# In_proj as 32x128 tiles beside ssm_out, one pair further ahead, with the first half's silus brought to their partitions by a staging tile and SBUF transfers

## The chip, the cores and the metric

The kernel runs on one NeuronCore of a Trainium2 chip, as one launch. The metric is device time in microseconds, the median of several executions. Before the change it is 1737.05 us (three runs, 1736.68 to 1737.44). Everything is float32.

## The reference

Four images x of 128 channels and 96x96 pixels are normalized in groups of four channels. Each is then read as four sequences of L = 9216: by rows, by rows backwards, by columns, by columns backwards. Every sequence goes through the same block (HID 256, MH 32, K 5, G 4):

```python
t = _grouped1x1(x, in_proj_w, in_proj_b, G)        # 128 -> 512 channels, 4 groups of 32 inputs
u, gate = (t[:, :HID], t[:, HID:])
u = jax.nn.silu(u)
u = lax.conv_general_dilated(u, dw_w, ...)          # depthwise, 5 taps
s = _conv1x1(u, ssm_in_w)                           # 256 -> 32
a = clip(DMIN + (DMAX - DMIN) * sigmoid(_conv1x1(u, ssm_delta_w, ssm_delta_b)), ...)
bb = tanh(_conv1x1(u, ssm_b_w, ssm_b_b)); cc = tanh(_conv1x1(u, ssm_c_w, ssm_c_b))
# h[l] = a[l] * h[l-1] + bb[l] * s[l], written with cumsums
u = u + _conv1x1(cc * hst + ssm_d[None, :, None] * s, ssm_out_w)     # 32 -> 256
u = _grouped1x1(u * jax.nn.sigmoid(gate), mix_w, mix_b, G)
return _conv1x1(u, out_proj_w, out_proj_b)          # 256 -> 128
```

The four results are put back in image order, joined to 512 channels, multiplied by fuse_w (512 to 128) and added to x. The kernel folds mix, out_proj and fuse into one matrix for each direction (w_fin), whose products it adds into the image, acc.

## The kernel before

**Order of work.** There are eight phases: four images, each once with columns as sequences (order V), once with rows (order H). A phase runs a sequence and its reverse together (s = 0, 1) in NS = 6 *steps* of 1536 positions, and a step in R = 4 *pairs*, one for each residue p of the position modulo 4, in the order TURN = 1, 2, 3, 0. So there are 192 pairs of 384 positions in two sequences; t numbers them, and a phase has 24. Since the second sequence is the first one backwards, the last three steps of a phase need the same in_proj and gates as the first three, mirrored. Only the first three are computed (fresh(step)); the others read what was kept, in SBUF (steps 3 and 4 use the silus of 2 and 1) or in DRAM (the gates, and the silus of step 0).

**A pair.** `pair_on(t)` writes the instructions of all engines by hand, in the order in which each engine runs them; the first six pairs have a function of their own, `pair(t)`. A pair holds, on TensorE: the depthwise conv of the first 128 channels as matmuls (`conv` with the matrices band, 128 rows by 32 columns, and in pairs of residues 1 and 2 also `conv_less`, 64 rows); two products with w_fin (`accumulate`) for a pair some seven back; the four ssm_out matmuls (`out_of`, L577) of the pair six back, 32 rows by 128 columns; and the projections to bb, cc, a and s (`proj`, 16 matmuls of 128 by 32). VectorE does the five taps of the other 128 channels (`taps`), the recurrence and the gating. GpSimd multiplies for the recurrence and adds into acc. ScalarE evaluates and copies out of PSUM.

**The front.** in_proj for four pairs ahead (a *front*, the g-th of the four of its step) stands at the start of a pair, `front(t + R, FRONT)`: for both sequences and both halves (j = 0, channels 0 to 127, for the conv; j = 1, the others, for the taps) four matmuls of 32 rows by 32 columns, 16 in all, and four silus (L527) into `sil`, whose first half has a residue on each 32 partitions. Column tile c of a matmul writes partitions 32c to 32c + 31 of the result; for j = 0 the four tiles are the four residues of channel group g, so the silus come out where the conv wants them; for j = 1 they are the four channel groups of residue g. Pairs with t modulo 24 from 20 to 7 hold a front; I call them *fronted*. The other twelve (8 to 19) hold the gates: four matmuls of 32 rows by 128 columns (`gate`, L557) between those of ssm_out, then a narrow tanh for each of two (L593, L599), and a wide one of both sequences.

**PSUM.** Eight banks. Taps and ssm_out use 0 to 3. In a gated pair conv uses 6 and 7, the products and projections 4 and 5 (PROJ). In a fronted pair the front uses 7, 6, 2, 3, conv 4 and 5, the products 7 and 6 (`banks, w`).

**Transfers.** Nearly all transfers are issued by SyncE, in the order of the program, each as soon as what it waits for is done; they go round eight semaphores, and one waits for the last transfer on its own. x_in is loaded for a front one step ahead (`load_front`), kept gates two pairs ahead (`load_kept`). `keep_lone` stores the outer residues of a step's silus (edge_sil), which `load_lone` brings back at the start of the step for `add_lone`. `keep_silu` (L507) stores the silus of step 0 for step 5. The pool gives `sil` two buffers, so step 2 takes that of step 0. `shared` has one buffer.

## Time and profile before

| | before |
|---|---|
| median of the runs | 1737.05 us |
| the profiled execution, its span | 1735.2 us |
| DMA engines busy, hardware queue 1 | 62.8% of 16 |
| moved | 363.66 MB, 210 GB/s |
| busiest TensorE groups | w_fin products 541.3 us, projections 535.0 us, conv 285.3 us, ssm_out 228.1 us, gates 161.7 us |
| silus, L527 | 384, 191.6 us, 584 ns each |

A profile shows one execution. TensorE's busy time counts pipelined matmuls, four of 32 columns side by side, so a busy TensorE can still hold pauses; how long a pair takes is better read between two starts of an instruction that comes once in each pair, as L781, the tanh of the projections.

### The profile page before, as it was taken

Reading aid. Unit: us, or ns where it says so; the run is one execution under the profiler, and the core shown is the slowest. Engines: PE = TensorE matmul, PEld = TensorE weight load, DVE = VectorE, ACT = ScalarE, POOL = GpSimd, SP = SyncE. Lnnn points to the kernel's source line nnn. Section 1 sums busy time; section 2 is a strip of 40 time slices with the busy share of each in tenths; the row PEclk is TensorE's granted clock in tenths of the full one; section 3 lists DMA queues with packets and bytes.
Section 4 is the critical chain, followed back from the end, with each engine's and each line's share of the span. In section 5 each row is a group of like instructions: output and inputs, shape, how many; then the busy total and the mean of one; then the engine's idle time right before and its main releaser. Section 6 shows DMA issues by size and latency. Waiting matters only on the chain.

```text
span 1735.2 us, 54226 instructions
## 1 busy us (share of the span) xinstructions
PE 1713.6 (99%) x22522; PEld 644.7 (37%) x22522; DVE 1507.9 (87%) x1508; ACT 1494.8 (86%) x2544; POOL 1447.0 (83%) x1490
## 2 busy tenths in 40 slices
PE   7999999999999999999999999999999999999998
PEld 4333333343333433344333443334333333333333
DVE  6899998888889998888889999888888888888887
ACT  4888988889888888888988888888998889888875
POOL 3689889888789988888788988887878889887887
PEclk9999999999999999999999999999999999999999
DMA  7746865358884786337896487433887548643364
GB/s 244 235 147 218 288 202 151 124 206 280 275 287 139 262 267 194 118 126 263 260 308 226 150 300 251 144 123 132 294 294 239 179 144 304 201 137 133 147 226 166
DMA packets 154644, 363.66 MB, mean 210 GB/s; under 512 B 19104, under 2 KB 120864, under 8 KB 154400
## 3 DMA queue, kind: packets, MB, share of 16 engines
q1 hardware_dynamic: 154256, 360.16, 62.8%
q8 instruction: 178, 2.92, 0.7%
q14 instruction: 66, 0.54, 0.1%
q10 hardware_dynamic: 144, 0.04, 0.0%
HBM read 221.41 MB, written 138.53 MB: 207 GB/s over the span
## 4 chain that ended last, share of the span: by engine, by line
PE 95%; DVE 2%; ACT 1%; DMA 1%; issue 0%; SPq 0%; DVEq 0%; ACTq 0%
PE psum L130 81%; PE psum L577 8%; PE psum L557 5%; DVE psum L744 1%; PE psum L1188 0%; DMA acc<-in_xr 0%; DMA kept<-shared 0%; DVE u L638 0%; ACT psum L589 0%; ACT psum L742 0%; DVE u L744 0%; ACT sil L527 0%; SPq L335 0%; PE psum L1195 0%; DVE u L691 0%
## 5 line engine op out<-in xcount | busy, mean ns | idle before, releaser
L744 DVE SCALAR_TENSOR_TENSOR psum<-sil,small,psum 128x768 f32<-128x768 f32 x576 | 589.1, 1023 | 42.2 <-ACT psum L742 16.8
L130 PE MATMUL psum<-u,w_fin 128*32 128x384 f32 (+1 forms) x6192 | 541.3, 484 | 1.1 <-ACT ys L860 0.4
L130 PE MATMUL psum<-u,main 128*32 128x384 f32 x6144 | 535.0, 489 | 0.5 <-DVE u L691 0.4
L638 DVE SCALAR_TENSOR_TENSOR u<-gate,psum 128x768 f32<-128x768 f32 x376 | 341.7, 950 | 150.0 <-PE psum L577 50.8
L879 POOL TENSOR_TENSOR acc<-ys,acc 128x384 f32<-128x384 f32 x375 | 411.8, 1120 | 14.0 <-ACT ys L860 1.9
L825 POOL TENSOR_TENSOR t<-t,t 64x384 f32<-64x384 f32 (+1 forms) x192 | 287.2, 1496 | 70.6 <-DVE t L819 48.3
L589 ACT COPY psum<-u 128x768 f32<-128x768 f32 x384 | 301.4, 799 | 10.5 <-DVE u L638 4.3
L130 PEld LDWEIGHTS psum<-u,w_fin 128*32 128x32 f32 x6192 | 195.2, 109 | 309.6 <-issue 235.5
L130 PEld LDWEIGHTS psum<-u,main 128*32 128x32 f32 x6144 | 180.0, 109 | 324.5 <-issue 218.3
L130 PE MATMUL psum<-sil,band 128*32 128x384 f32 x3072 | 285.3, 488 | 0.0
L792 POOL TENSOR_SCALAR t<-tm 64x384 f32<-64x384 f32 x184 | 170.8, 928 | 114.4 <-ACT tm L781 102.4
L826 POOL TENSOR_TENSOR t<-t,t 64x384 f32<-64x384 f32 (+1 forms) x192 | 233.9, 1218 | 15.1
L793 POOL TENSOR_TENSOR t<-t,tm 64x384 f32<-64x384 f32 x192 | 213.8, 1113 | 30.2 <-ACT t L784 15.5
L577 PE MATMUL psum<-t,main 32*128 32x384 f32 x1536 | 228.1, 525 | 4.2 <-ACT psum L589 4.2
L742 ACT ACTIVATE psum<-sil,small 128x768 f32<-128x768 f32 x191 | 172.6, 904 | 65.2 <-DVE u L638 61.9
L744 DVE SCALAR_TENSOR_TENSOR u<-sil,small,psum 128x768 f32<-128x768 f32 x192 | 194.9, 1015 | 6.8
L527 ACT ACTIVATE sil<-psum,bnorm 128x385 f32<-128x385 f32 x384 | 191.6, 584 | 4.0 <-DMA edge<-sil 0.9
L557 PE MATMUL psum<-x_in,wn 32*128 32x384 f32 x768 | 161.7, 498 | 0.0
L862 ACT COPY ys<-psum 128x384 f32<-128x384 f32 x288 | 132.3, 478 | 33.0 <-PE psum L130 28.3
L130 PEld LDWEIGHTS psum<-sil,band 128*32 128x32 f32 x3072 | 88.8, 108 | 171.4 <-issue 63.1
L781 ACT ACTIVATE tm<-psum,small 128x384 f32<-128x384 f32 x192 | 110.9, 578 | 14.0 <-PE psum L130 2.3
L577 PEld LDWEIGHTS psum<-t,main 32*128 32x128 f32 x1536 | 93.9, 183 | 73.7 <-issue 41.0
(108 smaller groups left out, 1512.3 us busy)
## 6 DMA issues: line engine op xcount, KB each, us to landing
gate<-kept SPq DMA_DIRECT2D x114, 768.0 KB, 5.2
kept<-gate SPq DMA_DIRECT2D x74, 768.0 KB, 3.7
sil<-sil SPq DMA_DIRECT2D x64, 770.0 KB, 6.6
lone<-edge SPq DMA_DIRECT2D x40, 770.0 KB, 7.5
x_in<-in_xs SPq DMA_DIRECT2D x250, 96.2 KB, 3.3
edge<-sil SPq DMA_DIRECT2D x96, 192.5 KB, 3.6
out<-acc SPq DMA_DIRECT2D x46, 384.0 KB, 6.4
acc<-in_xr SPq DMA_DIRECT2D x39, 384.0 KB, 6.4
```

The costliest lines, as they stand in the source:

```text
L130: nc.tensor.matmul(o[r, : rhs.shape[-1]], lhsT, rhs, start=start, stop=stop, skip_group_check=True)
L527: nc.scalar.activation(sils[step][:, s, j, g, :], bank(bk)[:, : N + 1], AF.Silu, bias=bn[:, 1:2] if j else bn[:, 4 + g : 5 + g],)
L557: nc.tensor.matmul(bank(to)[:, :N], stats[un["b"]][0][r, s, :], x_in[s][r, q, off : off + N], start=True, stop=True)
L577: nc.tensor.matmul(bank(ssm(bi, s) + j)[:, :N], w_so[r, bass.ts(j, P)], z[r, :], start=(bi, s) not in seeded, stop=True, skip_group_check= ...
L589: nc.scalar.copy(psum[:, ssm(bi, s) : ssm(bi, s) + 2, :N], us[bi][:, s])
L638: nc.vector.scalar_tensor_tensor(v, g, 1.0, pz, ALU.add, ALU.mult)
L742: nc.scalar.activation(part, src, AF.Copy, scale=w_tap[:, 0:1])
L744: nc.vector.scalar_tensor_tensor(us[i][:, :, 1, :] if k == K - 1 else part, src, w_tap[:, k : k + 1], part, ALU.mult, ALU.add,)
L793: nc.gpsimd.tensor_mul(ta[0:64, p, :], tb[0:64, :], tm[0:64, :])
L825: engine.tensor_mul(ta[0:64, p, r], tb[64:P, r], ta[64:P, p, r])
L826: engine.tensor_add(tb[0:64, r], ta[0:64, p, r], tb[0:64, r])
L879: adder.tensor_add(part, y, part)
```

## The change

In_proj leaves the start of the pair. `new_front` writes it as four matmuls of 32 rows by 128 columns, one for each sequence and half, in the places between the ssm_out matmuls where a gated pair has its gates, and for the pair five ahead (`ahead = t + R + 1`). With it the fronted pairs move by one: those with t modulo 24 from 19 to 6. The gates of a phase's first pairs are shared out again, two of them (no longer three) in the pairs 17 and 18 of the phase before. All pairs now use the banks of a gated pair.

For j = 1 a matmul gives the 128 channels of residue g where the taps want them, and two narrow silus (`new_silu`, L502) write `sil`. For j = 0 it gives all four channel groups of residue g on the four groups of partitions, and the conv wants the four residues there. So one wide silu of both sequences (`new_stage`, L515) writes a staging tile, and four transfers bring channel group m from partitions 32m of staging to partitions 32g of `sil`, at m. Staging has two slots, by g % 2, in the one buffer of `shared`, taken anew for each step. The edges are stored from staging, at g = 0 and g = 3, two transfers a step where `keep_lone` had four. The biases of the old layout and their spreading (`spread`) fall away. `keep_silu` of step 0 moves to the fronts of step 1, behind the transfers out of staging.

TensorE, pair 68 (phase 2, its step 5 begins), before. x_in is the input of in_proj, wn the normalized weights; the rows u, w_fin are the products, t, main ssm_out and u, main the projections:

```order
L130 MATMUL psum<-x_in_70,wn_2589 32x385 x8
L130 MATMUL psum<-x_in_71,wn_2589 32x385 x8
L130 MATMUL psum<-sil_6561,band 32x384 x8
L130 MATMUL psum<-u_3_2_0_6295,w_fin 32x384 x16
L130 MATMUL psum<-sil_6561,less 32x384 x8
L577 MATMUL psum<-t_2_3_3_0_6447,main 128x384 x4
L130 MATMUL psum<-u_5_1_0_6968,main 32x384 x16
```

and the same pair now:

```order
L130 MATMUL psum<-sil_6265,band 32x384 x8
L130 MATMUL psum<-u_3_2_0_5999,w_fin 32x384 x8
L130 MATMUL psum<-sil_6265,less 32x384 x8
L130 MATMUL psum<-u_3_2_0_5999,w_fin 32x384 x8
L490 MATMUL psum<-x_in_70,wn_2498 128x385
L622 MATMUL psum<-t_2_3_3_0_6151,main 128x384 x3
L490 MATMUL psum<-x_in_70,wn_2498 128x385
L490 MATMUL psum<-x_in_71,wn_2498 128x385
L622 MATMUL psum<-t_2_3_3_0_6151,main 128x384
L490 MATMUL psum<-x_in_71,wn_2498 128x385
L130 MATMUL psum<-u_5_1_0_6654,main 32x384 x16
```

The sixteen small matmuls at the start have become four among those of ssm_out.

SyncE, the end of pair 74 (t modulo 24 = 2, phase 3) and the first rows of the end of pair 75, in the changed kernel. L523 are the four pieces out of staging, L526 the edge, L552 the store of step 0's silus (sil_18 is step 0 of phase 3, sil_19 step 1, sil_20 step 2), L659 a load of kept gates; a row names the semaphores that it waits for, DMAHW those of transfers, and a transfer counts on the one that it waits for:

```order
L659 DMA gate0_176<-kept0_3_181 128x1536 [waits DMAHW4_49,DVE_49]
L523 DMA sil_19_6985<-shared_7010 32x2x385 [waits DMAHW5_49,Activation_49]
L523 DMA sil_19_6985<-shared_7010 32x2x385 [waits DMAHW6_49]
L523 DMA sil_19_6985<-shared_7010 32x2x385 [waits DMAHW7_49]
L523 DMA sil_19_6985<-shared_7010 32x2x385 [waits DMAHW0_49]
L526 DMA edge1_1_214<-shared_7010 128x2x385 [waits DMAHW1_49]
L552 DMA sil1_3_209<-sil_18_6598 128x1540 [waits DMAHW2_49]
L297 DMA x_in0_70<-in_xs 64x385 [waits DMAHW3_49,PE_49]
L297 DMA x_in1_71<-in_xs 32x385 [waits DMAHW4_49,PE_49]
L297 DMA x_in1_71<-in_xs 32x385 [waits DMAHW5_49,PE_49]
L659 DMA gate1_177<-kept0_2_180 128x1536 [waits DMAHW6_49,DVE_49]
```

The store of residue 3 stands behind the four pieces and the edge of that pair, on semaphore 2. Those of residues 1 and 2, in the pairs before, are on 7 and 0. Before the change the store stood in the fronts of step 0 itself, at the start of a pair and three pairs earlier.

ScalarE, pair 75 (t modulo 24 = 3), where step 2 begins, in the changed kernel. L634 and L907 are copies of the pair, L502 the narrow silus, L787 the first tap of the next pair, L515 the wide silu, L826 the tanh of the projections:

```order
L634 COPY psum_72<-u_2_5_2_0_6755 128x2x384 [waits DVE_49]
L907 COPY ys_2_5_1_1_7391<-psum_72 128x384 [waits PE_49]
L502 ACTIVATE sil_20_7393<-psum_72,bnorm_1_2499 128x385 [waits DMAHW2_49,DMAHW7_49,DMAHW0_49,PE_49]
L502 ACTIVATE sil_20_7393<-psum_72,bnorm_1_2499 128x385 [waits PE_49]
L787 ACTIVATE psum_72<-sil_19_6985,small_91 128x2x384 [waits DVE_49]
L515 ACTIVATE shared_7408<-psum_72,bnorm_1_2499 128x770 [waits DMAHW5_49,DMAHW4_49,DMAHW6_49,DMAHW1_49,DMAHW7_49,DMAHW0_49,Activation_49]
L826 ACTIVATE tm_3_0_0_0_7432<-psum_72,small_91 128x384 [waits PE_49,Pool_49]
```

Four silus at the start of the pair have become two narrow ones and a wide one between the gatings. The first of step 2 waits for the semaphores 2, 7 and 0.

The diff, cut to its core:

```diff
@@ pair(t), the first six pairs
-            front(t + R, FRONT if banks == PROJ else (5, 4, 2, 3))
+            spots = FRONT if banks == PROJ else (5, 4, 2, 3)
+            if t < R:
+                front(t + R, spots)
+            for f in {4: (8,), 5: (9, 10)}.get(t, ()):
+                to = (4, 5, 2, 3) if banks != PROJ else (6, 7, 2, 3)
+                one = new_front(f, to)
+                for x, y in ((0, 1), (0, 0), (1, 0), (1, 1)):
+                    one(x, y)
+                new_silu(f, to)
+                new_stage(f, to)
...
@@ the front
+    def new_front(i, banks):
+        step, g = divmod(i, R)
+        if g == 0:
+            sils[step] = new_sil(step)
+        st, r = step % NS, (0, 32, 64, 96)
+        def one(s, j):
+            q = R - 1 - g if s > j else g
+            a = slice(64 * s + 32 * j, 64 * s + 32 * j + 32)
+            nc.tensor.matmul(
+                bank(banks[2 * j + s])[:, : N + 1], stats[units[step * UB]["b"]][0][a, s, :], x_in[s][a, q, :],
+                start=True, stop=True,
+            )
+        return one
+
+    def new_silu(i, banks):
+        step, g = divmod(i, R)
+        bn = stats[units[step * UB]["b"]][1]
+        for s in range(2):
+            nc.scalar.activation(
+                sils[step][:, s, 1, g, :], bank(banks[2 + s])[:, : N + 1], AF.Silu, bias=bn[:, 1:2]
+            )
+
+    def new_stage(i, banks):
+        step, g = divmod(i, R)
+        st, bn, sil = step % NS, stats[units[step * UB]["b"]][1], sils[step]
+        if g == 0:
+            stages[0] = shared()[:, : 4 * (N + 1)].rearrange("p (e s n) -> p e s n", e=2, s=2)
+        stage = stages[0][:, g % 2]
+        nc.scalar.activation(
+            stage, psum[:, banks[0] : banks[0] + 2, : N + 1], AF.Silu, bias=bn[:, 0:1]
+        )
+        if st == 0:
+            nc.gpsimd.memset(stage[:, g // 2, 0:1], 0.0)
+            if g < 2:
+                nc.gpsimd.memset(sil[:, :, 1, g, 0:1], 0.0)
+        for m in range(4):
+            nc.sync.dma_start(sil[32 * g : 32 * g + 32, :, 0, m, :], stage[32 * m : 32 * m + 32, :, :])
+        if g in (0, R - 1):
+            e = 0 if g else 1
+            nc.sync.dma_start(
+                edge_of(step)[2 * e : 2 * e + 2].rearrange("a g c n -> (g c) a n"), stage
+            )
+        if st == 1 and step > 1:
+            keep_silu(step - 1, g)
+        if st < NS // 2 - 1:
+            load_front(step + 1, 0, slice(0, 64), slice(g, g + 1))
+            load_front(step + 1, 1, slice(64, 96), slice(R - 1 - g, R - g))
+            load_front(step + 1, 1, slice(96, P), slice(g, g + 1))
...
     def after_front(step, g):
...
-        if step and step % NS == 0:
-            keep_silu(step, g)
...
@@ pair_on(t)
-        fronted, gated = fresh(step), None
-        if mirror(n + 1) is None and (n + 1) % NP > 2:
+        ahead, gated = t + R + 1, None
+        if ahead * 2 >= NU or not fresh(ahead // R):
+            ahead = None
+        if mirror(n + 1) is None and (n + 1) % NP > 1:
...
-        banks, w = (PROJ, FRONT[:2]) if fronted else ((6, 7), PROJ)
+        banks, w = (6, 7), PROJ
...
-        front(t + R, FRONT)
+        mirrored(t + R)
...
+        spots = (6, 7, 4, 5)
+        if ahead is not None:
+            one = new_front(ahead, spots)
         def gate_of(s, j, bk):
             if gated is not None:
                 gate(2 * gated, s, j, bk)
+            elif ahead is not None:
+                one(1 - s, j)
...
+            elif s == 0 and ahead is not None:
+                new_silu(ahead, spots)
...
+        if ahead is not None:
+            new_stage(ahead, spots)
```

105 lines of the change are left out of this document (40 added, 65 removed).

## The prediction

> **What bounds the kernel now.** I read the page first, from its busy shares and its chain of waits:
>
> ```profile
> span 1735.2 us, 54226 instructions
> ...
> PE 1713.6 (99%) x22522; PEld 644.7 (37%) x22522; DVE 1507.9 (87%) x1508; ACT 1494.8 (86%) x2544; POOL 1447.0 (83%) x1490
> ...
> PE 95%; DVE 2%; ACT 1%; DMA 1%; issue 0%; SPq 0%; DVEq 0%; ACTq 0%
> ```
>
> TensorE is busy for 99% of the span and carries 95% of the chain that ended last. So a stage costs what TensorE's rounds cost plus every wait that lets TensorE stand, while the other engines have 13 to 17% to spare. The profiled execution took 1735.2 us against a median of 1737.05 us of the runs: 1.9 us more, which I add at the end.
>
> Next I read the busy time by stretches, with the starts of the projection's tanh (L781, once a pair) as borders. The first row is the six whole phases from pair 24 to pair 168, the second four fronted pairs (from pair 96), the last two four gated ones each (from pairs 104 and 32); the last column but one is the DMA engines' busy share:
>
> ```profile
> 237.36:1505.80 1268.44, 1267.80 (x16780) 472.32 (x16776) 1107.40 (x1077) 1124.10 (x1915) 1085.07 (x1114) 1.00 0.65 215
> 871.97:907.60 35.63, 35.63 (x516) 12.29 (x512) 31.25 (x33) 31.93 (x56) 28.67 (x29) 1.00 0.88 291
> ...
> 943.01:977.96 34.95, 34.95 (x424) 13.98 (x416) 32.65 (x33) 30.67 (x51) 32.24 (x29) 1.00 0.45 148
> ...
> 308.40:343.10 34.70, 34.70 (x420) 13.93 (x416) 29.98 (x29) 30.50 (x51) 28.30 (x28) 1.00 0.36 121
> ```
>
> Four fronted pairs take 35.63 us, four gated ones 34.70 or 34.95, although both hold the same number of matmul rounds: the 16 in_proj tiles of 32x32 are one round, the four gates of 32x128 another.
>
> **What the change removes.** By the order of TensorE's instructions a fronted pair now reads exactly like a gated one: four 32x128 matmuls between the four of ssm_out, in the same places and against the same banks. ScalarE's order is the gated pair's too, two narrow silus and a wide one where two narrow tanhs and a wide one stood. So the gated row prices it. Six phases are 36 groups of four: 36 x 34.70 = 1249.2 us, and the row has 1268.4, so 19.2 us lie in 72 fronted pairs, 0.27 us each. 85 pairs get an in_proj ahead: 22.7 us. Some gated groups take 34.95 us, which leaves less, so I take 21 us. Bounds: 0.17 us a pair (35.63 less 34.95, over four: 14 us) and 0.27 (23 us). Cover for the rest: ScalarE loses one activation a pair and VectorE nothing, both off the path. In the head one more front is made in pair 5, one round, under 1 us.
>
> **What it adds: transfers and one late wait.** Each front adds four transfers of 96 KB from staging to sil, and at residues 0 and 3 the edge copies leave from staging (384 KB each, before four of 192 KB once a step). The nearest rows are the page's DMA issues, with KB and median us to landing:
>
> ```profile
> gate<-kept SPq DMA_DIRECT2D x114, 768.0 KB, 5.2
> ...
> x_in<-in_xs SPq DMA_DIRECT2D x250, 96.2 KB, 3.3
> edge<-sil SPq DMA_DIRECT2D x96, 192.5 KB, 3.6
> ```
>
> The gated pairs give the times allowed, in the timeline of pairs 106 and 107 (start and length, us):
>
> ```profile
> 959.66 0.89 ACT L599 ACTIVATE gate<-psum,bnorm 128x768 f32<-128x768 f32 x1
> ...
> 965.72 0.58 ACT L593 ACTIVATE gate<-psum,bnorm 128x384 f32<-128x384 f32 x1 [0.33 <-PE psum L557]
> ...
> 967.92 0.89 ACT L599 ACTIVATE gate<-psum,bnorm 128x768 f32<-128x768 f32 x1
> ...
> 969.05 0.83 PE L130 MATMUL psum<-sil,band 128*32 128x384 f32 x8
> ```
>
> The wide activation, after which the staged pieces go out, ends at 960.55. From there 5.2 us pass to the next pair's first narrow activation (965.72), 7.4 to its wide one (967.92) and 8.5 to the conv after it (969.05), the first reader of a step's last pieces. SyncE's rows of pair 46 and the line view of the store of silus (L507) show how fast transfers are issued:
>
> ```profile
> 434.80 2.71 SPq L676 DMA_DIRECT2D edge<-sil  x4
> 437.61 0.55 SPq L507 DMA_DIRECT2D sil<-sil  x1
> ...
> L507 SPq DMA_DIRECT2D sil<-sil x32: 338/345/1399, 39.7 to 1494.9; - x32
> ...
> DMA to landing us min/median/max: 3.8/5.1/7.1
> ```
>
> Four issues take 1.4 to 2.7 us (0.34 each alone, 2.71 for the four edge copies). A piece lands 3.3 to 5.2 us behind its issue, so the last at 2 + 4 = 6 us of 8.5: hidden.
>
> The store of step 0's silus (keep_silu) is not. It moved from in front of a pair to behind the staging, and from the fronts of step 0 to those of step 1, since it must wait for the staged halves. Its last piece now leaves at the end of a pair t = 2 (mod 24). One pair on, at t = 3, step 2 begins, its tile takes step 0's buffer, and its first narrow silu (L502) waits for that store. In the order of ScalarE this silu names exactly the semaphores of those stores, in 7 of the 8 phases. Before, five pairs lay between. Behind the silu stand the first tap, the wide silu and the projection's tanh of ScalarE, and TensorE's projection, which needs the banks that the silus empty: a wait there is a wait of TensorE.
>
> How late is it? In the 5.2 us the store must be issued and land. Ahead of the store stand four staged pieces and an edge copy. Five issues take 1.7 to 3.4 us; I take 2.5. Landing is 3.8 to 7.1 us after issue; behind a gate load, 384 KB of pieces and a 384 KB edge I take 6.4, near the store above that had four edges ahead. Wait: 2.5 + 6.4 - 5.2 = 3.7 us; bounds 2.5 + 3.8 - 5.2 = 1.1 and 2.5 + 7.1 - 5.2 = 4.4. That holds for the four phases of order H (1, 3, 5, 7), where DMA is light (0.50 in the first row below, pairs 24 to 27): 4 x 3.7 = 15 us.
>
> The three V phases that follow another image (2, 4, 6) are crowded: outputs leave and the next image loads. The rows behind the first are pairs 47 to 50, into phase 2:
>
> ```profile
> 237.36:273.30 35.94, 35.94 (x536) 12.38 (x528) 30.63 (x32) 31.11 (x57) 32.07 (x37) 1.00 0.50 153
> ...
> 439.40:448.73 9.33, 9.33 (x140) 3.19 (x136) 8.01 (x8) 8.41 (x15) 8.28 (x8) 1.00 1.03 319
> 448.73:458.00 9.27, 9.27 (x140) 3.13 (x136) 7.72 (x8) 8.42 (x16) 6.78 (x8) 1.00 1.04 357
> 458.00:466.52 8.52, 8.52 (x124) 2.98 (x120) 7.78 (x10) 7.55 (x14) 8.06 (x9) 1.00 0.62 232
> 466.52:475.04 8.52, 8.52 (x124) 2.98 (x120) 7.75 (x10) 7.55 (x14) 5.57 (x6) 1.00 0.84 223
> ```
>
> and, of the first two, the landing of a gate load:
>
> ```profile
> issues: line engine op xcount, KB each, median us to landing
> gate<-kept SPq DMA_DIRECT2D x3, 768.0 KB, 7.7
> ```
>
> Two stretches are full (1.03 and 1.04) at a mean of 338 GB/s. Each now gets 384 KB of pieces and a 770 KB store more, the first also an edge of 384 KB: 2.7 MB, 8 us at that rate. The third has 0.38 x 8.5 = 3.2 us free and gets 3.4 us of work. So the store of the last piece can be 8 us later than in an H phase: 3.7 + 8 = 11.7 us. The least is a store that meets only the landing times of full stretches (7.7 us), with no backlog in front: 2.5 + 7.7 - 5.2 = 5.0. I take 8.5, the middle, since shares over 1 say that transfers overlap: 3 x 8.5 = 25 us.
>
> The staging tile has one buffer, too. The wide silu of residue 0 waits for the pieces and the edge of residue 3, one pair before. At t = 23 that pair's pieces also wait for GpSimd's memset, which stands behind two accumulations (one pair's rows):
>
> ```profile
> 900.92 1.97 POOL L879 TENSOR_TENSOR acc<-ys,acc 128x384 f32<-128x384 f32 x2
> ...
> 907.43 1.96 POOL L879 TENSOR_TENSOR acc<-ys,acc 128x384 f32<-128x384 f32 x2
> ```
>
> The second ends at 909.4, 1.8 us behind the tanh L781 that starts at 907.60, about when the wide activation ends. Pieces and edge are issued by 1.8 + 2.5 = 4.3 us and land 3.6 us later, at 7.9; a pair gives 7.4. Some 0.5 us, seven times: 3 us, bounds 0 and 9.
>
> Sum: 1735.2 - 21 + 15 + 25 + 3 = 1757; with the 1.9 us of the median, **1759 us**.
>
> **A rule weighed.** The store is 770 KB, and its quickest landing was 3.8 us. By the Trainium skill (DMA: Bandwidth & Descriptors, Anatomy of one DMA) a DMA costs about 2.0 us plus its bytes over 436 GB/s, an estimate of 3.8 us here (a fit of transfers that GpSimd issues). By that price every boundary would cost 1.1 us and the change would gain: the second rival's time. The row's median of 5.1 us speaks against it, since a transfer that stands behind others takes their time too.
>
> **Rivals.** First, *the same wait, and TensorE's clock falls in it.* TensorE stood for 11.66 us at the start, and its first matmuls then went slowly:
>
> ```profile
> 11.66 5.49 PE L1188 MATMUL psum<-acc 128*128 128x512 f32 x6 [11.66 <-DMA acc<-in_xr]
> ...
> 18.05 0.57 PE L1188 MATMUL psum<-acc 128*128 128x192 f32 x2
> ```
>
> 5.49 us for 3 x 512 columns (each recorded twice) is 3.6 ns a column, against 0.57/192 = 3.0: 0.9 us lost at least, since the small ones' fixed part weighs more. At 1.3 us a wait, seven add 9 us: 1768. For it: the waits last a third of that first idle, or nearly all of it. Against: no idle in the steady part shows it. The Trainium skill (TensorE: Matmul & The Clock Gate, The HAM clock gate) puts the threshold at an idle window of about 3.4 us, so the crowded boundaries would pay and the light ones perhaps.
>
> Second, the other side: *the store lands in time.* Place: L502 at t = 3; it decides when the store's mean landing falls under some 5.7 us, where seven waits eat the 21 us. At 3.8 us each wait is 1.1 us, 8 in all: 1737 - 21 + 8 = 1724. For it: the fastest of 32 stores. Against: those had no five transfers just ahead.
>
> Third, *the wait is not met at all*, because ScalarE is itself late by then: the gain alone, 1716. It would have to be 4 us late in each fresh half, and the gated rows show it waiting for TensorE (0.33 us).
>
> Fourth, *transfers flood every fronted pair*: the conv of steps 0 to 2 waits as well, and the crowded boundaries cost 12 us or more with loads of gates late. 3 x 12 + 15 + 10 - 21 = +40: 1777. For it: shares of 1.03. Against: 0.65 over the six phases.
>
> **How the numbers follow.** Forecast 0.5, clock 0.2, flood 0.12, store in time 0.10, gain alone 0.03, waits and gain equal 0.05. The forecast's own range, from the bounds: least waits 4 + 15 + 0 less 21 gives 1735, most 18 + 35 + 9 less 21 gives 1778. The rival of the clock is inside; to leave out no more than 2 in 10 I take 1734 to 1782. Slower by over 0.2% (3.5 us, about what a measurement of this kernel can tell from none): 0.82; faster 0.13; within 0.05.
>
> **What would show it.** In the changed profile: fronted stretches without a boundary at 34.7 to 34.9 us a group (the gain); L502 preceded by idle ended by a DMA sil<-sil or by the semaphore of one, seven times, 3 to 5 us in H phases and 5 to 12 in V phases; the store's landing at 6 us or more; L515 idle at t = 23 under 1 us; no conv waiting for sil<-shared. A granted clock under 1.00 behind the waits would be the first rival. Wrong would be: no idle before L502, or group times of 35.6 as before.

## The result and the profile after

The changed kernel takes 1822.09 us (median of four runs, 1819.75 to 1827.23), 1.0496 times the kernel before (interval 1.048 to 1.0513): 85 us slower. The prediction said slower, at 1759 us, and gave 1734 to 1782 as its range: the sign is right, the size is not.

The page of the changed kernel, its span, busy shares, chain and TensorE clock (each digit of that row a fortieth of the span, in tenths):

```profile
span 1818.8 us, 50579 instructions
...
PE 1722.7 (95%) x20410; PEld 696.8 (38%) x20410; DVE 1523.4 (84%) x1508; ACT 1481.6 (81%) x2414; POOL 1450.7 (80%) x1462
...
PEclk9999999999899999999989999899998999999999
...
PE 80%; DMA 9%; ACT 3%; DVE 2%; SPq 2%; issue 2%; POOL 1%; ACTq 0%; POOLq 0%; DVEq 0%
```

TensorE's share of the chain fell from 95% to 80%, and transfers hold 9%, where they held 1%. Every engine's share fell: the kernel waits. The busy time by stretches, first the same six whole phases (pairs 24 to 167) and then the same four fronted pairs from pair 96, gives the place:

```profile
240.06:1582.42 1342.36, 1274.65 (x15048) 515.42 (x15048) 1118.77 (x1077) 1112.64 (x1807) 1087.27 (x1089) 0.97 0.71 220
904.17:955.84 51.67, 37.89 (x420) 14.57 (x416) 32.20 (x33) 31.34 (x52) 29.39 (x30) 0.83 0.96 296
```

The six phases take 73.9 us more than before (1268.44), the four pairs 51.67 instead of 35.63 us, with a granted clock of 0.83 and the DMA engines busy for 0.96. The group list names what ScalarE waited for, and the line view of the store of silus (L552) how long that took to land:

```profile
L502 ACT ACTIVATE sil<-psum,bnorm 128x385 f32<-128x385 f32 x176 | 101.6, 582 | 118.7 <-DMA sil<-sil 55.1
...
ACT sil L502 <- DMA sil<-sil: 55.1, 6, 15.8
...
ACT sil L502 <- DMA x_in<-in_xs: 16.5, 1, 16.5
...
DMA to landing us min/median/max: 4.7/7.6/9.3
```

Seven waits of the narrow silu, 71.6 us in all, at t = 3 of phases 1 to 7. The first four pairs of these phases take 79.7 us more than before (between the starts of the tanh), all the rest of the kernel 3.9 us more. One wait is booked on a load of x_in, which the silu does not read; the transfer that was last by the profile need not be the one that counted. Phase 1, in ScalarE's and TensorE's timelines and SyncE's queue:

```profile
256.55 0.89 ACT L515 ACTIVATE shared<-psum,bnorm 128x770 f32<-128x770 f32 x1
...
268.73 1.05 ACT L502 ACTIVATE sil<-psum,bnorm 128x385 f32<-128x385 f32 x2 [6.42 <-DMA sil<-sil]
...
269.37 5.35 PE L130 MATMUL psum<-u,main 128*32 128x384 f32 x32 [5.92 <-ACT sil L502]
...
257.47 2.53 SPq L523 DMA_DIRECT2D sil<-shared  x4
260.04 0.59 SPq L526 DMA_DIRECT2D edge<-shared  x1
260.68 0.49 SPq L552 DMA_DIRECT2D sil<-sil  x1
```

The pieces leave when the wide activation has ended (257.4), the store 3.2 us later; the silu starts 8.0 us after that. And in phase 2, where the tanh L826 starts as the wide activation ends:

```profile
475.78 0.57 ACT L826 ACTIVATE tm<-psum,small 128x384 f32<-128x384 f32 x1
...
496.62 1.05 ACT L502 ACTIVATE sil<-psum,bnorm 128x385 f32<-128x385 f32 x2 [15.82 <-DMA sil<-sil]
...
484.34 3.17 SPq L523 DMA_DIRECT2D sil<-shared  x4
487.55 0.59 SPq L526 DMA_DIRECT2D edge<-shared  x1
488.19 0.48 SPq L552 DMA_DIRECT2D sil<-sil  x1
```

SyncE reached the pieces 8.5 us after they were ready: it was a pair behind. The projections behind the wait in phase 1 took 5.35 us, in a pair without one 2.77:

```profile
306.92 2.77 PE L130 MATMUL psum<-u,main 128*32 128x384 f32 x32
```

The stretches behind the two waits show why, with the granted clock in the last column but two:

```profile
269.40:274.80 5.40, 5.40 (x36) 1.74 (x40) 4.08 (x4) 2.60 (x5) 0.89 (x1) 0.50 0.26 61
275.00:283.30 8.30, 8.30 (x108) 3.05 (x104) 6.21 (x4) 7.12 (x12) 7.67 (x6) 1.00 0.52 153
...
497.30:500.10 2.80, 2.80 (x20) 0.94 (x24) 1.56 (x2) 1.99 (x3) 0.00 (x0) 0.50 1.03 357
```

TensorE ran at half speed for 5.4 us in the one and 2.8 us in the other. By the same view of the other five waits it was 4.4 to 6.0 us there, 35.5 us for all seven; half of that is lost, an estimate of 18 us. The Trainium skill (TensorE: Matmul & The Clock Gate, The HAM clock gate) says that the array falls to half speed after an idle window of about 3.4 us and comes back after a busy one of that length. The trace agrees that it falls in a wait and comes back in work: in all seven waits, of 4.3 to 16.0 us on TensorE, the clock fell. It does not show the length: the fall came 1.9 us (phase 3) to 4.9 us (phase 6) after TensorE's last matmul, and the return 2.9 to 6.0 us after its next.

### The profile page after: what moved, and what is told of

Same layout as the page of the kernel before. It is cut to its first block, busy times and chain, and to the rows that moved or that the text cites. A ratio compares the mean times of both kernels' runs of the same rounds, so it can differ in the third digit from the quotient of the medians.

```text
span 1818.8 us, 50579 instructions
## 1 busy us (share of the span) xinstructions
PE 1722.7 (95%) x20410; PEld 696.8 (38%) x20410; DVE 1523.4 (84%) x1508; ACT 1481.6 (81%) x2414; POOL 1450.7 (80%) x1462
## 4 chain that ended last, share of the span: by engine, by line
PE 80%; DMA 9%; ACT 3%; DVE 2%; SPq 2%; issue 2%; POOL 1%; ACTq 0%; POOLq 0%; DVEq 0%
PE psum L130 65%; PE psum L622 6%; PE psum L602 5%; DMA sil<-sil 4%; PE psum L490 4%; SPq L523 2%; DMA edge<-shared 1%; DMA gate<-kept 1%; DMA x_in<-in_xs 1%; DVE psum L789 1%; DMA sil<-shared 1%; DVE t L864 1%; ACT psum L787 1%; DVE u L683 1%; ACT tm L826 1%
## 5 line engine op out<-in xcount | busy, mean ns | idle before, releaser
L130 PE MATMUL psum<-u,main 128*32 128x384 f32 x6144 | 551.4, 501 | 68.7 <-ACT sil L502 68.2
L130 PE MATMUL psum<-u,w_fin 128*32 128x384 f32 (+1 forms) x6192 | 551.9, 485 | 1.1 <-ACT ys L905 0.5
L924 POOL TENSOR_TENSOR acc<-ys,acc 128x384 f32<-128x384 f32 x375 | 423.6, 1151 | 12.5 <-ACT ys L905 1.9
L870 POOL TENSOR_TENSOR t<-t,t 64x384 f32<-64x384 f32 (+1 forms) x192 | 277.8, 1447 | 66.2 <-DVE t L864 38.0
L634 ACT COPY psum<-u 128x768 f32<-128x768 f32 x384 | 306.2, 798 | 7.2 <-DVE u L683 4.4
L622 PE MATMUL psum<-t,main 32*128 32x384 f32 x1536 | 272.1, 519 | 3.7 <-ACT psum L634 3.7
L838 POOL TENSOR_TENSOR t<-t,tm 64x384 f32<-64x384 f32 x192 | 219.5, 1143 | 36.8 <-ACT t L829 22.5
L871 POOL TENSOR_TENSOR t<-t,t 64x384 f32<-64x384 f32 (+1 forms) x192 | 233.2, 1215 | 15.1
L502 ACT ACTIVATE sil<-psum,bnorm 128x385 f32<-128x385 f32 x176 | 101.6, 582 | 118.7 <-DMA sil<-sil 55.1
L787 ACT ACTIVATE psum<-sil,small 128x768 f32<-128x768 f32 x191 | 172.0, 901 | 14.9 <-DVE u L683 12.2
L907 ACT COPY ys<-psum 128x384 f32<-128x384 f32 x288 | 137.9, 479 | 53.9 <-PE psum L130 44.6
L130 PEld LDWEIGHTS psum<-sil,band 128*32 128x32 f32 x3072 | 102.3, 110 | 161.1 <-issue 80.3
L490 PE MATMUL psum<-x_in,wn 32*128 32x385 f32 x704 | 150.4, 500 | 1.1 <-ACT sil L502 0.7
L864 DVE TENSOR_TENSOR_SCAN t<-t 64x768 f32<-64x768 f32 x56 | 123.3, 2202 | 12.1 <-POOL t L838 10.5
```

What stands on the lines that cost most here:

```text
L130: nc.tensor.matmul(o[r, : rhs.shape[-1]], lhsT, rhs, start=start, stop=stop, skip_group_check=True)
L490: nc.tensor.matmul(bank(banks[2 * j + s])[:, : N + 1], stats[units[step * UB]["b"]][0][a, s, :], x_in[s][a, q, :], start=True, stop=True,)
L622: nc.tensor.matmul(bank(ssm(bi, s) + j)[:, :N], w_so[r, bass.ts(j, P)], z[r, :], start=(bi, s) not in seeded, stop=True, skip_group_check= ...
L634: nc.scalar.copy(psum[:, ssm(bi, s) : ssm(bi, s) + 2, :N], us[bi][:, s])
L787: nc.scalar.activation(part, src, AF.Copy, scale=w_tap[:, 0:1])
L838: nc.gpsimd.tensor_mul(ta[0:64, p, :], tb[0:64, :], tm[0:64, :])
```

## The experiments

My first theory was the prediction's: the late store makes the waits, the clock falls in them, and nothing else of weight was added. The rival: transfers are late in general, and the store is only where that is paid. All times are medians of runs beside the kernel before (1736.8 to 1737.7 us).

### Take the store away, or move it

Three kernels differ from the changed one by the place of one line in `new_stage`. In the first, `keep_silu` is left out but for phases 0 and 1; in the second it stands ahead of the staged pieces; in the third it is issued two at a time, for g = 0 and 1 in pair 23 and for 2 and 3 in pair 0.

```
-        if st == 1 and step > 1:
-            keep_silu(step - 1, g)                      # behind the pieces and the edge
+        if st == 1 and step > 1:                        # ahead of the pieces; first run: if step == NS + 1
+            keep_silu(step - 1, g)                      # second run
+            for h in {0: (0, 1), 1: (2, 3)}.get(g, ()): # first and third run
+                keep_silu(step - 1, h)
```

> The changed kernel with the store of step 0's silus left out in six of the seven phases (kept for phases 0 and 1 only, and in phase 1 issued two at a time in pairs t = 23 and 0, ahead of the staged pieces). Phases 2 to 7 thus read old silus in their step 5: that part of the computation is left wrong. My theory (the silu L502 at t = 3 waits for that store, TensorE's clock falls behind the wait, and nothing else of weight was added): the seven excesses at t = 3 (73.6 us in all) and at t = 4 (13.0 us) go; 1822 - 84 = 1738 us, within 5. Rival (the transfers out of staging flood the queues, and the store is only where the lateness is paid): the waits turn up at other DMA-fed instructions, and the time stays above 1775 us.

> The changed kernel with the store in the same pairs, but ahead of the four staged pieces and the edge in SyncE's order instead of behind them. My theory (place in the queue decides in H phases, SyncE's own lateness in V phases): in phases 1, 3, 5, 7 the store leaves 3.2 to 3.8 us earlier and lands in 5 to 6.5 us instead of 7.9, so the four waits of 5 to 8 us shrink to under 1 us each (-24 us, and -4 us of half clock); in phases 2, 4, 6, where SyncE is already a third of a pair late, some 5 us of each wait of 15 go and 10 stay. Together 1775 us, 1768 to 1785. Rival (the pieces ahead are the whole cause): 1740 us, no waits at all. Rival (the place in the queue is nothing, the pair of the store is all): 1810 us or more.

> The changed kernel with all four stores kept, issued two at a time in pairs t = 23 and t = 0 ahead of the staged pieces, so two to three pairs before the tile is taken again. My theory: no wait at t = 3 and no half clock, 1740 us (1736 to 1745), level with the kernel before, since the 21 us of gain were also eaten by waits of 0.3 to 1.4 us at t = 0, 8, 20 and 23 that this does not touch. Rival (those small waits come from the same late queue): 1716 to 1728 us, faster than the kernel before. Rival (the flood of transfers): above 1775 us.

Measured: 1771.37, 1799.13 and 1793.32 us. Each helps, none as far as the theory said (1738, 1775 and 1740); even with nearly no store, 34 us stay. The first lies 4 us under what the rival said too (above 1775); the third came out as the rival said. In the second run SyncE reached the gate load ahead of the store at 260.80 only, so that the store still left after the wide activation's end (260.3); and behind the wait for it stood a second one, that of the wide silu for its staging tile (SyncE and ScalarE, phase 1):

```profile
260.80 0.35 SPq L659 DMA_DIRECT2D gate<-kept  x1
261.20 0.42 SPq L552 DMA_DIRECT2D sil<-sil  x1
...
259.42 0.89 ACT L515 ACTIVATE shared<-psum,bnorm 128x770 f32<-128x770 f32 x1
...
268.69 1.05 ACT L502 ACTIVATE sil<-psum,bnorm 128x385 f32<-128x385 f32 x2 [3.51 <-DMA sil<-sil]
...
271.82 0.90 ACT L515 ACTIVATE shared<-psum,bnorm 128x770 f32<-128x770 f32 x1 [1.28 <-DMA edge<-shared]
```

In the third run the silu L502 no longer waits for its buffer, and the waits have moved (TensorE's list, then VectorE and ScalarE in phase 2):

```profile
PE psum L130 <- ACT shared L515: 46.9, 18, 11.0
...
489.69 0.56 DVE L437 BATCH_NORM_STATS2 bn<-xs 128x6 f32<-128x384 f32 x1 [9.50 <-DMA xs<-in_xr]
490.17 1.80 DVE L684 SCALAR_TENSOR_TENSOR u<-gate,psum 128x768 f32<-128x768 f32 x2
...
491.14 0.91 ACT L788 ACTIVATE psum<-sil,small 128x768 f32<-128x768 f32 x1 [7.55 <-DVE u L684]
495.68 0.90 ACT L515 ACTIVATE shared<-psum,bnorm 128x770 f32<-128x770 f32 x1 [3.63 <-DMA x_in<-in_xs]
```

ScalarE's first tap (L788) waited for VectorE's gating (L684), and that stood behind a BATCH_NORM_STATS2 (statistics for the normalization) which had waited 9.50 us for xs, a chunk of the next image that SyncE loads; four such waits take 17.6 us in this run, two waits of the gating itself for gate loads 4.7. The wide silu then waited for its staging tile, thus for transfers out of it; the row books that on the transfer that came last, a load of x_in. So the theory of the store alone falls: two more things were covered by its wait, loads that come late and the staging tile.

### Staging once a phase

```
-        if g == 0:
+        if g == 0 and (st == 0 or step < NS):
             stages[0] = shared()[:, : 4 * (N + 1)].rearrange(...)
```

Taken anew, the tile waits for all transfers of its last holder, thus for the pair before; taken once, each slot waits for its own, two pairs back. (On the kernel of the third run.)

> The kernel of the early store, with the staging tile taken once a phase instead of anew at each step, so that the wide silu of residue 0 waits for the transfers of its own slot (two pairs back) and no longer for those of the pair before. My theory now (two causes add up at the boundaries: the reuse of buffers that transfers still read, and transfers that are late because the queue is full): at t = 3 the part of the wait that L515 showed goes (3.6 us in phases 2, 4, 6; 1.5 in 1, 3, 5, 7), and most of the 1 us at t = 23 and 0; the rest, VectorE's gating waiting for a gate load that landed 9.7 us after its issue, stays: 1793 - 17 - 8 = 1768 us, 1760 to 1778. Rival (the transfers are merely late, and the next reader, the conv, pays): 1785 us or more. Rival (the reuse is the whole rest): 1740 us.

Measured: 1772.30 us (1.0198, 1.0173 to 1.0223), 21 us less, inside what was expected. The wait that the prediction had put at 3 us was worth 21 once the store's was gone. What is left stands where a new image begins: the first four pairs of phases 2, 4 and 6 take 11.1, 11.3 and 7.4 us more than before, those of the other phases 2.1 at most. VectorE waits for chunks there in phases 2 and 4 (14.5 us in two waits), and now the conv itself waits for pieces:

```profile
PE psum L130 <- DMA sil<-shared: 13.6, 4, 6.6
...
PE psum L130 <- ACT shared L515: 7.8, 8, 3.0
```

### Less to carry at the boundaries

The next image's chunks (192 KB each, two in every third and fourth pair of four in the V phases) go to pairs 8 to 17; the control does the same to the kernel before.

```
-        places = singles * 2
...
+        places = [ph * NP + t for t in [*range(8, 18)] * 2 + [10, 11, 14, 15]]
```

> The kernel of the run with staging once a phase, and with the next image's statistics (loads xs and bn_stats, 4.6 MB per V phase) moved from the third and fourth pair of every four to pairs 8 to 17 of the phase, out of the pairs 19 to 6 where the fronts are made and the DMA engines were busy for 0.9 to 1.05. If a full queue is what makes the gate loads late, they land in time: the excesses at t = 2, 3 and 4 of phases 2, 4, 6 fall under 2 us each, 1738 to 1746 us. Rival (the pieces' own number and order on SyncE, not the bytes, make the lateness): within 5 us of the run without this move. Rival (VectorE, given more in the gated pairs of the V phases, slows those): 8.3 and 9.1 us pairs become longer by 0.4 each, no gain.

> The kernel before with the statistics moved in the same way: the control for the run above. By the theory of the full queue the old kernel had no wait there, so no change: 1737 us, within 3. Rival (the move pays for itself, since the crowded pairs of the old kernel were longer too): 1725 to 1733 us. Rival (VectorE becomes the bound in the gated pairs): above 1742 us.

Measured: 1776.43 us (interval 1.02 to 1.0241, not told from the run before it, where 1738 to 1746 was expected) and 1747.12 us for the control (1.0052, 1.0037 to 1.0067), where no change was expected. The control was needed: the move alone costs the old kernel 9 us. Its pairs t = 8, 12 and 16 of the V phases took 10.0 to 10.2 instead of 9.1 to 9.3 us (from the tanh of the pair before to its own), and ScalarE's first tap waited for VectorE's gating 10 times and 9.5 us more than in the kernel before (first row), where it had two bn_stats more to do:

```profile
ACT psum L742 <- DVE u L638: 61.9, 86, 1.7
```

```profile
ACT psum L740 <- DVE u L636: 71.4, 96, 1.7
```

So this pair of runs says little of the queue.

### The change without its transfers

From phase 2 on no piece is sent, and sil lies in two fixed places, so that the conv has old data to read. (On the kernel with staging once a phase.) The first kernel leaves out the late stores of step 0 too, the second keeps them, early.

```
-        for m in range(4):
+        for m in range(4 if step < 2 * NS else 0):
             nc.sync.dma_start(sil[32 * g : 32 * g + 32, :, 0, m, :], stage[...])
...
+        if of != "last" and of >= 2 * NS:                 # in new_sil
+            return sils[7 if of % 12 in (0, 2, 5, 7) else 11]
```

> What the change is worth without its transfers: the kernel with staging once a phase, where from phase 2 on the four transfers from staging to sil and the store of step 0's silus are left out (sil lies in two fixed places there, and the conv's half of it keeps old silus: that part of the computation is left wrong). In_proj, the silus, the staging activation, the edges and all other loads are as in the changed kernel. If the 21 us of gain are real on TensorE and only the transfers hide them, phases 2 to 7 run at the gated pairs' times but for the 1 us at t = 0 of phases 3, 5, 7 and 0.4 at t = 8, which come from VectorE's and ScalarE's steps of the next image's statistics (BATCH_NORM_AGGREGATE between a scan and the gating): 1728 us, 1722 to 1734. Rival (the gain never was there, TensorE's rounds cost the same): 1737 to 1742 us. Rival (the late transfers have another cause than these): above 1750 us.

> The run without pieces (1734 us) with the stores of step 0's silus put back in all phases, two at a time in pairs 23 and 0 (the stored first halves are old, as there). If pieces and store only together fill the queue: within 3 us of 1734, since the old kernel had this store, and moved 28 MB less than the changed one. If the store by itself makes loads late: 1745 us or more.

Measured: 1734.19 and 1733.75 us, both 0.9981 of the kernel before (0.9972 to 0.9991 and 0.9971 to 0.9991). The store alone costs nothing. The fixed places of sil are no part of the difference that can be seen: with staging once a phase, the narrow silu waited for transfers only 0.6 us in all, without the store not at all. And the gain was 3 us, not 21, nor the 9 that the first run's expectation still hoped for. The stretches of the second, six phases and the four fronted pairs from pair 96:

```profile
241.21:1501.51 1260.30, 1258.80 (x15048) 505.76 (x15048) 1115.93 (x1077) 1112.99 (x1807) 1084.64 (x1089) 1.00 0.65 214
871.46:906.64 35.18, 35.18 (x420) 13.96 (x416) 31.58 (x33) 31.38 (x51) 28.76 (x29) 1.00 1.03 328
```

Six phases gain 8.1 us (from 1268.44), four fronted pairs 0.45 (from 35.63) and not the 0.68 to 0.93 of the gated rows. Besides, counted from the tanh of the pair before, t = 0 of phases 1, 3 and 5 takes 0.7 us more than before and t = 8 of each phase 0.4, some 4 us over the six phases. At t = 0 VectorE's BATCH_NORM_AGGREGATE stands ahead of the gating, and ScalarE's first tap, wide silu and tanh now stand behind that; what is late at t = 8 was not followed. VectorE and ScalarE in pair 72:

```profile
658.52 0.81 DVE L236 BATCH_NORM_AGGREGATE mv<-bn 128x2 f32<-128x144 f32 x1
659.25 1.75 DVE L686 SCALAR_TENSOR_TENSOR u<-gate,psum 128x768 f32<-128x768 f32 x2
...
660.18 0.91 ACT L790 ACTIVATE psum<-sil,small 128x768 f32<-128x768 f32 x1 [0.81 <-DVE u L686]
```

The pairs up to the first 24, which still have their pieces, take 3.7 us more (203.4 us from the first tanh to that of pair 24, before 199.7).

### Pieces: bytes, packets or number

Three ways. First, the order of sil's axes is changed so that a piece is 32 packets of 3080 bytes, not 64 of 1540 (same bytes); and on it, the chunks moved to pairs where VectorE has room:

```
-        return t.rearrange("p g s j n -> p s j g n")
...
+        return t.rearrange("p g j s n -> p s j g n")
...
-        places = singles * 2
+        places = [ph * NP + t for t in [6, 7, 10, 11, 14, 15, 18, 9, 13, 17] * 2 + [10, 11, 14, 15]]   # the second only
```

> The kernel with staging once a phase, with the order of sil's axes changed so that a staged piece is 32 rows of 3080 bytes instead of 64 of 1540 (same bytes, same four transfers a front, half the packets). If the DMA engines' time sets the lateness (a 1540-byte packet took 66 to 91 ns, a 3072-byte one 121 to 145), nothing much changes: 1765 to 1775 us. If the number of packets sets it (the issue of a piece took SyncE 0.60 us, 2.4 us a pair), the issue of a piece falls to 0.35, SyncE wins 1 us in each fronted pair, and the pieces land in time in phases 1, 3, 5 and 7: 1748 to 1762 us.

> The kernel of the long packets, with the statistics of the next image moved out of the fronted pairs as in the earlier run, but now to pairs where VectorE has room (second, third and fourth of each four; the first ones had become 1 us longer). By the theory of a full queue (1.2 MB fewer in the stretch before each of three boundaries, 3 to 4 us of all engines' time): 8 to 12 us below the run of the long packets, with the gated pairs unchanged. Rival (the stretch is bound by the eight transfers in flight and the order on SyncE, and what is taken away makes no room): within 4 us of it.

Measured: 1776.55 us (1.0192 to 1.0242), not told from the 1772.30 of the short packets; 1765.14 us with the chunks moved (1.0138 to 1.018), 11 us less, as expected. Halving the packets of a piece gained nothing. Moving the chunks took away two waits of BATCH_NORM_STATS2 for them (15.7 us in all); the gating now waits 12.8 us in four for gate loads, where it waited 6.8.

Then the pieces without the store, and from the kernel of the stores alone, half the bytes sent in two ways: one sequence of each piece (four transfers of 48 KB), or two whole pieces (of 96 KB).

```
-            nc.sync.dma_start(sil[32 * g : 32 * g + 32, :, 0, m, :], stage[32 * m : 32 * m + 32, :, :])
+            h = slice(0, 2 if step < 2 * NS else 1)      # half the bytes, range(4)
+            nc.sync.dma_start(sil[32 * g : 32 * g + 32, h, 0, m, :], stage[32 * m : 32 * m + 32, h, :])
...
+        for m in range(4 if step < 2 * NS else 2):       # half the number
```

> The kernel with staging once a phase (1772 us), without the store of step 0's silus from phase 2 on (those steps 5 read old silus: left wrong), the staged pieces kept. If store and pieces share the cost (the store of 3.1 MB a phase against 13 pairs of 0.4 MB pieces), it lies halfway to the run without both: 1750 to 1757 us. If the pieces are the whole cost: 1768 or more. If the store is: 1736 to 1742.

> Stores as in the run of the stores alone, and from phase 2 on each staged piece carries one of the two sequences only (48 KB instead of 96): four transfers a front, half the bytes; the other half of the conv's silus stays old, that part is left wrong. To be held against the next run, which halves the bytes by sending two whole pieces of four. If bytes (packets' time on the DMA engines) set the lateness, the two agree within 3 us, at about 1748. If the number of transfers does (eight in flight at a time, 0.6 us of SyncE for an issue), this one is over 5 us slower than the next: 1752 to 1765.

> As the run of half the bytes, but with two whole pieces of 96 KB a front instead of four halves of 48 KB (the other two channel groups stay old: left wrong). If bytes set the lateness: within 3 us of it, about 1748. If the number of transfers does: over 5 us faster than it, 1738 to 1746.

Measured: 1756.04, 1762.63 (1.0135 to 1.0165) and 1751.71 us (1.0065 to 1.0102). The first lies in the range of a shared cost, the second in that of the number of transfers; the third is 6 us above its own (1738 to 1746), but the two are apart by more than the 5 us that were to decide. Pieces alone cost 22 us over the run without both, pieces and store 38. At equal bytes four transfers cost 11 us more than two, and halving the bytes at four was worth 10 at most (against 1772.30, which also takes sil's places anew). The four pairs 48 to 51 at the start of phase 2 show it best; the rows are those of half the bytes, of half the number, and of the stores alone:

```profile
456.99:503.28 46.29, 38.60 (x420) 16.02 (x416) 31.50 (x33) 31.31 (x52) 30.87 (x31) 0.89 0.88 282
```

```profile
459.26:500.95 41.69, 37.00 (x420) 15.05 (x416) 31.52 (x33) 31.31 (x51) 30.34 (x31) 0.96 1.00 307
```

```profile
451.36:486.42 35.06, 35.06 (x420) 14.06 (x416) 31.65 (x33) 31.34 (x51) 28.85 (x29) 1.00 1.05 338
```

The slowest has the DMA engines least busy (0.88, at 282 GB/s); the fastest moves most per microsecond. So the engines' time alone is not what bounds the slower ones. What fits is SyncE's order: it issues in order, each transfer takes the next of eight semaphores in turn, and waits there until the transfer that had it before has landed. SyncE's list of waits, in the run of four half pieces and in the run of two, names that:

```profile
SPq L297 <- DMA sil<-sil: 36.3, 20, 3.2
SPq L297 <- DMA gate<-kept: 18.4, 18, 2.8
```

```profile
SPq L297 <- DMA gate<-kept: 7.2, 7, 1.8
...
SPq L297 <- DMA sil<-sil: 5.0, 3, 2.0
```

The loads of x_in (L297), issued behind the pieces, waited 55 us for landings of transfers that they do not depend on, and 12 us with two pieces fewer. Other lines took over part of it in the second run (over all lines, SyncE's waits for landings were 122 and 100 us), so these rows fit the mechanism without proving it; the times give its price. Much of it was paid by VectorE, where BATCH_NORM_STATS2 in phases 2 and 4 waited for a chunk that SyncE loads, in the two runs:

```profile
DVE bn L437 <- DMA xs<-in_xr: 16.3, 2, 8.3
...
DVE bn L437 <- DMA xs<-in_xr: 8.7, 2, 5.4
```

With the stores alone that wait was 0.6 us. TensorE's conv waited for pieces too, 17.7 and 4.0 us; in the second run it has two pieces fewer to wait for, which is a rival to their number in SyncE's order. The next runs leave the pieces alone.

### The same at equal bytes, without leaving work out

On the kernel with staging once a phase, the loads of x_in for the next step are joined, three after every second front instead of three after each; and then the chunks are moved as well.

```
-        if st < NS // 2 - 1:
-            load_front(step + 1, 0, slice(0, 64), slice(g, g + 1))      # and two more
+        if st < NS // 2 - 1 and g % 2:
+            load_front(step + 1, 0, slice(0, 64), slice(g - 1, g + 1))  # and two more
```

> The kernel with staging once a phase (1772 us), with the loads of x_in for the next step joined: three transfers after every second front (two residues each) instead of three after each. Same bytes and packets, 1.5 transfers fewer a front; nothing else changed. By the number of transfers (two fewer a front took 11 us off the run of half the bytes): 8 us less, 1764, and less in phases 2, 4 and 6. By bytes: 1772 us, within 3; or more, since a joined transfer comes later for the residue that was loaded first.

> As the run before, and the next image's statistics moved out of the fronted pairs to those where VectorE has room (11 us in the earlier pair of runs): 1764 - 11 = 1753 us if the two add up; still slower than the kernel before, since the staged pieces keep SyncE late. Rival (both take the same lateness away): 1760 us or more. Rival (the queue falls under what eight transfers in flight carry, and the lateness goes at once): 1738 or less.

Measured: 1761.34 us (1.0111 to 1.0164), 11 us under the same bytes in more transfers (1772.30, 1.0173 to 1.0223), a little more than the 8 expected, with the same pieces for the conv to wait for; and 1756.02 us (1.0099 to 1.0133), which the intervals do not tell from 1761. This is the best version with nothing left out, and it is still 1.2% slower than the kernel before. What is left cannot pay: even with no pieces the gain was 3 us.

## Why the prediction was wrong, step by step

| step of the prediction | it said | measured |
|---|---|---|
| fronted pairs become like gated ones | -21 us | -3 (without pieces, 1733.75) |
| staged pieces to conv | hidden, 0 | +38 (to 1772.30, with the early store) |
| staging tile's reuse | +3 | +21 (1772.30 to 1793.32); 5.9 us of waits in the changed kernel |
| store of step 0's silus | +40 | +29 (1793.32 to 1822.09); 71.6 us of waits |

The rows on the right are steps of one path from 1737 to 1822 us; since the waits cover each other, another order would share them out otherwise (taking the store out alone gave 51 us).

**The step that failed** is "a piece lands 3.3 to 5.2 us behind its issue, so the last at 2 + 4 = 6 us of 8.5: hidden". The landing itself was right in the median, 4.5 us in the changed kernel, though up to 10.3, and there TensorE never waited for a piece. But the step asked only whether the reader gets its data in time. Four transfers more in each fronted pair, and in two of four an edge behind them, do not only arrive: they stand in SyncE's order ahead of the loads of x_in, of the next gates and of the next image's chunks, and take four or five of the eight semaphores. At the boundaries SyncE falls a pair behind, as the 8.5 us of phase 2 show, and what it issues there is late. The prediction did work out a backlog for the crowded V phases, but by bytes (2.7 MB at 338 GB/s, 8 us), and gave it to the store alone.

**The store's wait** was right in place, in the instruction that waits and in number: L502, at t = 3, seven times. Its size was not: 3.7 us were expected in an H phase, where the quoted one is 6.42 (issue 3.2 us behind the wide silu instead of 2.5, and 8.0 to the silu's start instead of 6.4), and 8.5 in a V phase (15.82). The four waits of the H phases and the three of the V phases made 71.6 us where 15 + 25 were forecast, and the half clock behind them some 18 more. The 8.0 us lie above the longest landing that was taken for a bound, 7.1 us from the old kernel's stores; the median landing of the new ones was 7.6. The estimate of 3.8 us from the Trainium skill (DMA: Bandwidth & Descriptors, Anatomy of one DMA) was still further off, as the prediction had thought.

**The staging tile's reuse** was priced at t = 23 alone. There it was 0.8 to 1.5 us in five phases, not 0.5 in seven. It stands at t = 3 as well, where the queue is latest, as the 3.63 us above show. That its bound of 9 was too low for the same reason as the pieces' zero fits this, but no run separates it.

**The gain** came out below its lower bound even without pieces: 8.1 us in the six phases, where 0.17 us for each of 72 fronted pairs makes 12.2, and 3 us over the kernel. A gated row does not price a fronted pair: a group without pieces took 35.18 us, not 34.70 to 34.95; VectorE's steps for the next image fall into pairs where ScalarE's work now stands behind them; and the pairs up to the first 24 lost 3.7 us, where under 1 was allowed for the head.

**The rivals.** The clock (chance 0.2) came true as an addition, some 18 us by the estimate above against 9; it is inside the steps of the table. The flood (0.12, 1777) named the right fact, that loads come late and the conv waits too, beside the main one and not in its place; it did not name the chunks. The flood's 61 us, 3 for staging and 9 for the clock, less the measured gain of 3, make 1807 us: the rivals were treated as alternatives, though nothing kept them apart. That the store lands in time, or is not met, is excluded by the seven waits.

**What it said would show it** held for the seven waits, the landing over 6 us and the clock, and for no conv waiting on pieces, which showed only once the first two waits were away. It failed for the size of the waits, for L515 at under 1 us, and for the groups at 34.7 to 34.9 us: the pairs 4 to 7 of phases 1 to 7, behind the boundary, took 35.2 to 35.5 us, as before (35.3 to 35.5).

## What to carry to other kernels

Price a transfer that is added to a full queue by what stands behind it on its issuing engine, not by its own landing: count transfers per pair against how many may be in flight, look for every reader of what comes late, here VectorE's statistics of the next image too, and join what can be joined before cutting bytes. When one wait is found, ask which others it covers; here each that was taken away showed the next, 29, 21 and 38 us. A gain that is read from another stage's time should first be measured without the new cost, as the run without pieces did: it would have ended the idea at 3 us.

## What was not expected of the hardware

Halving the bytes of the pieces left the DMA engines less busy in the four pairs above (0.88 against 1.00) and the kernel 11 us slower than halving their number. Nor did the issue depend on size: four pieces took SyncE 2.53 us in the changed kernel (above), 2.42 at half the bytes, 2.43 at half the packets:

```profile
485.75 2.42 SPq L529 DMA_DIRECT2D sil<-shared  x4
```

```profile
1563.53 2.43 SPq L528 DMA_DIRECT2D sil<-shared  x4
```

The Trainium skill (DMA: Bandwidth & Descriptors, Bandwidth) advises large batches, with 64 KB as the size under which descriptors dominate. This case agrees that fewer and larger transfers are better at equal bytes (the joined loads of x_in, 11 us); the packet's length, doubled in pieces of 96 KB, gained nothing.

What stays open: how the 38 us of pieces split between SyncE's order and its eight semaphores. Another issuing engine was not tried, since ScalarE is busy for 31.38 us of the 35.18 that four fronted pairs take without pieces, and GpSimd for 28.76; sixteen issues of 0.6 us, as SyncE's rows have them, would be an estimated 9.6 us more.
